# Identity products in TensorE's waits, fewer transposes on TensorE, and a planner with measured transfer figures

## The chip, the cores and the metric

The kernel runs on one core of a Trainium2 chip. The metric is the device time of one execution in microseconds (us). A profile's span is some 2 us shorter than the device time of the same execution, so spans are compared with spans and times with times. In the profile's lines PE is TensorE (matmuls), PEld its loading of weights, DVE is VectorE, ACT ScalarE, POOL GpSimd and SP the engine that issues most of the transfers; L295 is line 295 of that kernel. PSUM holds the tiles that this kernel's matmuls write; the program keeps eight of them and calls them banks.

## The reference

Four graph layers run one after the other on 32 graphs of 512 nodes and 128 features, all in FP32. Each layer normalises x, applies a ReLU, multiplies by the graph's 512 x 512 matrix or its transpose, and adds to x. Cut to what matters:

```python
h = maximum(layernorm(x), 0); x = x + L0(h, adj)   # one linear map, adj scaled by degrees
h = maximum(layernorm(x), 0); x = x + L1(h, adj)   # two aggregations (adj and adj.T), elu, tanh
h = maximum(layernorm(x), 0); x = x + L2(h, adj)   # four such layers; adj normalised by rows and by columns
h = maximum(layernorm(x), 0); x = x + L3(h, adj)   # a message step, then a GRU cell
return x
```

## The kernel before

The kernel is written as a list of operations for each graph ("batch"), and a planner in Python fixes one order for all engines before the program is built. The planner simulates the engines and the DMA queue with a duration for each operation, and starts on each engine the ready operation with the earliest due time.

The parts that the change touches are these. How a transfer is reckoned, and when a batch is due:

```python
PERIOD = 28.0                     # us from one batch's due time to the next one's
RATE, TRANSFER = 240.0, 1.3       # bytes per ns of the queue; us to landing
...
if kb:                            # op(): a transfer of kb thousand bytes
    o.us, o.land = max(us, kb / self.RATE), self.TRANSFER + land
...
due = o.batch * PERIOD if o.batch < B - 1 else (B - 2) * PERIOD + ENDING
o.key = (due - o.tail + o.later if o.rank is None else o.rank - 1e6, i)
```

The reserve of PSUM banks: an operation of a batch may take a new bank only if this many are left for each older unfinished batch:

```python
older = item[1].batch - min(unfinished)
if any(len(free[x.kind]) < ... + older * self.kept.get(x.kind, 0) for x in new):
    held.append(item); continue
...
plan = Plan(sb, psum, {"bank": 8, ...}, {"bank": 1, ...})
```

How h is turned (128 features on partitions in place of 128 nodes). In most batches VectorE transposes in blocks (0.71 us for a tile of 128 x 512 in the trace) and the tile goes out to memory and back in another order. In the first three and the last two batches TensorE does it, sixteen transposes of 128 x 128 a batch:

```python
at_ends = b < 3 or b >= B - 2

def transposed(h, name):
    if at_ends:
        for c in range(NC): ... nc.tensor.transpose(ps[:, c*P:(c+1)*P], h[:, c, :], ident)
        ... nc.scalar.copy(hT, ps)
        return hT
    t = turned(h, "turned")       # VectorE block transpose, four stores of 64 KB, a load of 256 KB
    ... nc.scalar.copy(hT, t in order)
```

And the spreading of the norms over all partitions:

```python
op("SP", 0.4, bounced, [inv], [bounce], kb=128)
op("SP", 0.4, spread, [bounce], [spaced], kb=512)       # DMA, 512 KB
op("ACT", t_act(2 * N), lambda: nc.scalar.copy(rows..., spaced...), [spaced], [rows])
```

At the end all operations are emitted in the planned order: `for o in plan.order(): o.emit()`.

## Time and profile before

| | before |
|---|---|
| device time, median of 3 (range) | 2331.95 us (2329.25 to 2332.02) |
| span of the profile, mean clock | 2328.9 us, 0.997 |
| TensorE busy | 2293.4 us |
| first real matmul | at 11.06 us |

The lines that matter are shown in the prediction below. They say that TensorE is the bound, that it is practically without a gap between 60 and 2180 us, and that what can be won lies in the first 60 us and around 2188 us. One line of TensorE's waits is added here: the group that waited, what released it, then us in total, times, and the longest. (Line numbers differ a little between kernels, since the edits add lines.)

```profile
PE ps_t L483 <- ACT h L447: 5.1, 3, 3.1
```

The three waits of the transposes for the normalised h (5.1 us, one of them 3.1) are the largest after the wait for the first weights. TensorE's clock in that trace: from the first matmul at 11.06 us to 16.46 us 25 records took 5.40 us, 0.216 each, where 12 later ones took 1.34 (21.72 to 23.06), 0.112 each; the granted clock was at half from 30.11 to 33.52 and from 54.00 to 60.83 us, then full to 2323.87 us.

To follow where time goes I cut each span into six pieces that add up to it, by my own count over TensorE's records in the traces. A record of 128, 256, 384 or 512 columns is typically followed by the next one 0.112, 0.216, 0.325 or 0.429 us later. The sum of these over all records that do real work is "real". Everything beyond is counted as lost where it occurs: in the start (before 60 us, after the first real matmul), the middle (60 to 2160 us) and the end. A product of the identity is counted wholly as lost. Before: 11.1 first matmul + 2279.9 real + 18.9 start + 4.3 middle + 7.2 end + 7.7 tail (last record to the end of the span), in sum 2329.1 (the last record's own spacing, 0.1 to 0.3, is in both real and tail).

### The profile page before, as it was taken

Reading aid. Unit: us, or ns where it says so; the run is one execution under the profiler, and the core shown is the slowest. Engines: PE = TensorE matmul, PEld = TensorE weight load, DVE = VectorE, ACT = ScalarE, POOL = GpSimd, SP = SyncE. Lnnn points to the kernel's source line nnn. Section 1 sums busy time; section 2 is a strip of 40 time slices with the busy share of each in tenths; the row PEclk is TensorE's granted clock in tenths of the full one; section 3 lists DMA queues with packets and bytes.
Section 4 is the critical chain, followed back from the end, with each engine's and each line's share of the span. In section 5 each row is a group of like instructions: output and inputs, shape, how many; then the busy total and the mean of one; then the engine's idle time right before and its main releaser. Section 6 shows DMA issues by size and latency. Waiting matters only on the chain.

```text
span 2328.9 us, 28035 instructions
## 1 busy us (share of the span) xinstructions
PE 2293.4 (98%) x9594; PEld 1438.1 (62%) x9594; DVE 1519.9 (65%) x4124; ACT 935.0 (40%) x2018; POOL 284.2 (12%) x218
## 2 busy tenths in 40 slices
PE   6999999999999999999999999999999999999998
PEld 4666666566665666666666666666656666666565
DVE  5556567666676776757766676666667667576754
ACT  7323434344343444434444333443434444344512
POOL 3001101111110111101111011111011111011101
PEclk9999999999999999999999999999999999999999
DMA  6202222323323133222233223232231332323100
GB/s 215 81 1 86 68 74 81 109 64 100 98 83 109 46 109 104 90 87 82 78 104 100 74 90 109 64 100 91 80 116 50 109 96 91 94 64 113 50 5 10
DMA packets 127295, 196.63 MB, mean 84 GB/s; under 512 B 18352, under 2 KB 75184, under 8 KB 127152
## 3 DMA queue, kind: packets, MB, share of 16 engines
q1 hardware_dynamic: 126864, 194.71, 27.2%
q8 instruction: 76, 1.25, 0.2%
q14 instruction: 67, 0.55, 0.1%
q10 hardware_dynamic: 288, 0.13, 0.0%
HBM read 157.95 MB, written 36.83 MB: 84 GB/s over the span
## 4 chain that ended last, share of the span: by engine, by line
PE 91%; DVE 3%; issue 2%; DMA 2%; ACT 1%; POOL 1%; SPq 0%; DVEq 0%; POOLq 0%; ACTq 0%
PE ps_agg L295 60%; PE ps_seven L566 12%; PE ps_sd L295 9%; PE ps_upd L295 3%; PE ps_gate L295 2%; PE ps_msg L295 1%; PE ps_lin L295 1%; PE ps_node L295 1%; DMA x<-in_x 0%; POOL inv L690 0%; ACT h L447 0%; DVE bn L419 0%; SPq L465 0%; DMA turned<-turn_turned 0%; DVE z L637 0%
## 5 line engine op out<-in xcount | busy, mean ns | idle before, releaser
L295 PE MATMUL ps_agg<-aT,sd 128*128 128x512 f32 x1024 | 509.6, 593 | 1.8 <-DVE sd L544 1.0
L295 PE MATMUL ps_agg<-a,sd 128*128 128x512 f32 x1024 | 489.4, 593 | 0.0
L435 POOL TENSOR_TENSOR sc<-v,neg_half 128x4 f32<-128x4 f32 (+1 forms) x128 | 170.0, 1328 | 1630.8 <-DVE v L422 1053.3
L295 PEld LDWEIGHTS ps_agg<-a,sd 128*128 128x128 f32 x1024 | 181.7, 190 | 158.3 <-issue 148.8
L447 ACT ACTIVATE h<-xr,nb,sc 128x128 f32<-128x128 f32 x384 | 158.2, 482 | 294.0 <-DVE nb L443 290.2
L295 PE MATMUL ps_agg<-f,w_sb 128*128 128x512 f32 x448 | 229.4, 594 | 0.0
L295 PEld LDWEIGHTS ps_agg<-aT,sd 128*128 128x128 f32 x1024 | 177.5, 191 | 75.1 <-issue 62.0
L295 PE MATMUL ps_sd<-w_sb,f 128*128 128x256 f32 x768 | 221.6, 381 | 1.8 <-ACT f L485 1.3
L566 PEld LDWEIGHTS ps_seven<-t_sb,s 128*128 128x128 f32 x1128 | 164.2, 191 | 67.9 <-issue 56.2
L295 PEld LDWEIGHTS ps_sd<-w_sb,f 128*128 128x128 f32 x768 | 137.5, 192 | 107.4 <-issue 85.0
L522 DVE TENSOR_TENSOR sd<-ps_sd,rf_sb 128x512 f32<-128x512 f32 x128 | 88.2, 689 | 145.2 <-PE ps_sd L295 144.5
L566 PE MATMUL ps_seven<-t_sb,s 128*128 128x128 f32 x1128 | 177.2, 275 | 0.0
L737 ACT ACTIVATE f<-ps_agg,cf_sb 128x512 f32<-128x512 f32 x128 | 87.4, 683 | 145.3 <-PE ps_agg L295 145.0
L295 PE MATMUL ps_agg<-aT,rep 128*128 128x512 f32 x256 | 130.9, 593 | 2.6 <-DVE rep L662 1.4
L295 PE MATMUL ps_agg<-a,rep 128*128 128x512 f32 x256 | 130.7, 592 | 0.0
L295 PE MATMUL ps_agg<-aT,msg 128*128 128x512 f32 x256 | 127.6, 593 | 0.0
L566 PEld LDWEIGHTS ps_seven<-w_sb,f 128*128 128x128 f32 x512 | 83.5, 191 | 55.7 <-issue 47.1
L690 POOL TENSOR_TENSOR inv<-stat,neg_half 128x8 f32<-128x8 f32 x32 | 64.7, 2022 | 370.5 <-DVE stat L689 370.5
L592 DVE TENSOR_TENSOR ev<-ps_seven,ev 128x512 f32<-128x512 f32 x94 | 64.6, 688 | 65.0 <-PE ps_seven L566 63.5
L607 ACT ACTIVATE sq<-a 128x512 f32<-128x512 f32 x128 | 79.9, 624 | 51.7 <-DMA a<-in_adj 50.3
L295 PE MATMUL ps_agg<-aT,h 128*128 128x256 f32 (+2 forms) x384 | 99.7, 380 | 0.0
L295 PEld LDWEIGHTS ps_agg<-f,w_sb 128*128 128x128 f32 x448 | 78.4, 191 | 27.8 <-issue 20.3
(142 smaller groups left out, 3781.9 us busy)
## 6 DMA issues: line engine op xcount, KB each, us to landing
aT<-in_adjt SPq DMA_DIRECT2D x124, 512.0 KB, 5.7
a<-in_adj SPq DMA_DIRECT2D x62, 512.0 KB, 5.5
turn_turned<-blk SPq DMA_DIRECT2D x324, 64.0 KB, 1.8
turned<-turn_turned SPq DMA_DIRECT2D x81, 256.0 KB, 2.7
spaced<-bounce SPq DMA_DIRECT2D x32, 512.0 KB, 4.8
x<-in_x SPq DMA_DIRECT2D x32, 256.0 KB, 2.8
out<-xo SPq DMA_DIRECT2D x30, 256.0 KB, 2.1
turn_f4r<-blk SPq DMA_DIRECT2D x108, 64.0 KB, 1.8
```

The costliest lines, as they stand in the source:

```text
L295: op("PE", t_mm(n), lambda: nc.tensor.matmul(out_of(ps.ap()), lhs(), rhs(), start=start, stop=stop), reads, [ps], later=later)
L435: op("POOL", t_pow(n), lambda: nc.gpsimd.tensor_tensor(inv.ap()[:, :n], v8.ap()[:, :n], neg_half[:, :n], op=ALU.pow), [v8, NH], [(inv, {0})])
L447: op("ACT", t_act(D, 2), lambda c=c: nc.scalar.activation(h.ap()[:, c, :], xin.ap()[:, c, :], AF.Relu, bias=nb.ap()[:, c:c + 1], scale=inv ...
L522: op("DVE", t_tt(N), lambda ps=ps, h=h: nc.vector.tensor_add(sd.ap()[:, 2 * h:2 * h + 2, :], ps.ap().rearrange("p (j v) -> p j v", j=2), s ...
L566: op("PE", t_mm(D), lambda j=j: nc.tensor.matmul(ps.ap()[:, k * H + j * D:k * H + (j + 1) * D], lhs()[:, j * P:(j + 1) * P], rhs(), start= ...
L592: op("DVE", t_tt(N), lambda: nc.vector.tensor_add(ev.ap(), bank_b.ap()[:, None, :H].to_broadcast([P, 2, H]), ev.ap()), [bank_b, ev], [ev])
L607: op("ACT", 0.73, lambda c=c: nc.scalar.activation(sq.ap(), a.ap()[:, c, :], AF.Copy, accum_out=stat.ap()[:, c:c + 1]), [(a, {c})], [sq, ( ...
L690: op("POOL", t_pow(2 * NC), lambda: nc.gpsimd.tensor_tensor(inv.ap(), stat.ap(), neg_half, op=ALU.pow), [stat, NH], [inv])
L737: op("ACT", t_act(N, 1), lambda ps=ps, i=i, f_new=f_new: nc.scalar.activation(f_new.ap(), ps.ap(), AF.Tanh, bias=cf_sb[:, i:i + 1]), [ps, ...
```

## The change

The intent: (1) where the planner foresees a wait of TensorE of over 0.7 us, products of the identity with itself are put into it, as many as it should hold, so that the clock stays up; (2) batches 2 and 30 are turned by way of VectorE and memory and no longer on TensorE; (3) the planner's figures for transfers are taken from the trace (it reckons 400 bytes per ns for the queue in place of 240, where the trace before has 404 to 411 GB/s between 10 and 20 us; and for a load 1.5 us plus its size at 175, which is 3.0 us for a turned tile of 256 KB, where that trace has a median of 2.7), batches are 30 us apart in place of 28, and two PSUM banks are reserved for each older batch in place of one.

```diff
-PERIOD = 28.0
+PERIOD = 30.0
...
-    RATE, TRANSFER = 240.0, 1.3
+    RATE, ALONE, TRANSFER, ISSUE = 400.0, 175.0, 1.5, 0.45
...
         if kb:
-            o.us, o.land = max(us, kb / self.RATE), self.TRANSFER + land
+            o.us = max(self.ISSUE, kb / self.RATE)
+            o.land = self.TRANSFER + kb / self.ALONE - o.us
...
+    WARM, COLD, RISE, SHORT = 0.2225, 0.428, 3.5, 0.7
+
+    def kept_warm(self, done, product, begin):
+        banks = {x for o in done for x in o.bufs if x.kind == "bank"}
+        out, at, cold = [], begin, self.RISE
+        for o in done:
+            if o.engine == "PE":
+                gap = o.ready - at
+                if gap > self.SHORT:
+                    n = int(min(gap, cold) / self.COLD + max(gap - cold - 0.1, 0.0) / self.WARM)
+                    cold = 0.0
+                    used = {x.slot for x in banks if x.since < o.ready and x.until > at - 0.1}
+                    slot = next((k for k in range(self.places["bank"]) if k not in used), None)
+                    if slot is not None:
+                        out.append((slot, n))
+                at = o.ready + o.us
+            out.append(o)
... (then emits them; a pair (slot, n) becomes n products)
-    plan = Plan(sb, psum, {"bank": 8, ...}, {"bank": 1, ...})
+    plan = Plan(sb, psum, {"bank": 8, ...}, {"bank": 2, ...})
...
-        at_ends = b < 3 or b >= B - 2
+        at_ends = b < 2 or b >= B - 1
...
+    def idle_products(slot, n):
+        ps = psum.tile([P, N], F32, name="ps_idle", tag=f"bank_{slot}", bufs=1)
+        for _ in range(n):
+            nc.tensor.matmul(ps[:, :P], ident, ident, start=True, stop=True)
...
-        for o in plan.order():
-            o.emit()
+        plan.kept_warm(plan.order(), idle_products, 1.3)
```

## The prediction

> **What bounds the kernel now.** I read the table of busy time first, then the slices, then the sums by stretch, and last TensorE's own list in order of time for the two stretches where it idles.
>
> ```profile
> PE 2293.4 (98%) x9594; PEld 1438.1 (62%) x9594; DVE 1519.9 (65%) x4124; ACT 935.0 (40%) x2018; POOL 284.2 (12%) x218
> ...
> PE   6999999999999999999999999999999999999998
> ...
> PE 91%; DVE 3%; issue 2%; DMA 2%; ACT 1%; POOL 1%; SPq 0%; DVEq 0%; POOLq 0%; ACTq 0%
> ```
>
> TensorE is busy for 2293.4 of 2328.9 us, only the first and last slices are not full, and 91% of the chain that ended last is matmuls. Nothing off TensorE can be worth much by itself. All that is left outside TensorE's busy time is 2328.9 - 2293.4 = 35.5 us, 1.5% of the span. The sums by stretch say where these lie (columns: stretch, its length, then busy time and instructions of PE, PEld, DVE, ACT, POOL, then granted clock, DMA share, GB/s):
>
> ```profile
> 0.00:60.00 60.00, 39.13 (x185) 29.45 (x186) 30.96 (x126) 43.08 (x112) 17.59 (x21) 0.92 0.62 214
> 60.00:2180.00 2120.00, 2117.03 (x8852) 1324.28 (x8850) 1407.62 (x3784) 851.82 (x1818) 250.23 (x175) 1.00 0.28 85
> 2180.00:2196.00 16.00, 13.43 (x50) 7.88 (x50) 10.39 (x37) 8.85 (x18) 5.45 (x4) 1.00 0.41 118
> 2196.00:2300.00 104.00, 102.67 (x402) 60.95 (x402) 53.38 (x127) 17.26 (x32) 2.01 (x2) 1.00 0.03 8
> 2300.00:2329.00 29.00, 21.14 (x107) 15.56 (x106) 17.58 (x53) 14.00 (x43) 8.88 (x17) 0.91 0.07 19
> ```
>
> The first 60 us hold 20.9 us of idle TensorE, the 2120 us after them only 3.0, the 16 us around 2188 hold 2.6, the next stretch 1.3, and the tail 7.9. The last is mostly the gate arithmetic and the store after the last matmul (ended at 2321.5 us). The clock is under full only at the two ends. In TensorE's list in order of time of the first 60 us (start, duration, what, idle before):
>
> ```profile
> 11.06 2.93 PE L295 MATMUL ps_fold<-raw 128*128 128x128 f32 x12 [11.06 <-DMA raw<-in_raw]
> ...
> 30.00 3.68 PE L295 MATMUL ps_sd<-w_sb,hT 128*128 128x256 f32 x8 [0.75 <-ACT hT L485]
> ...
> 55.43 1.63 PE L483 MATMUL ps_t<-ident,h 128*128 128x128 f32 x4 [3.07 <-ACT h L447]
> ```
>
> and of the stretch near the end:
>
> ```profile
> 2182.34 1.48 PE L483 MATMUL ps_t<-ident,h 128*128 128x128 f32 x4 [0.65 <-ACT h L447]
> ...
> 2191.39 1.89 PE L295 MATMUL ps_sd<-w_sb,hT 128*128 128x256 f32 x8
> ```
>
> The last line is the same eight records as those at 30.00: 1.89 us here, 3.68 us there. That is the clock: the early eight came after two waits and ran at half rate.
>
> [...] The cold stretch at 30 us does follow a stretch of transposes and waits, but this trace does not part the two. [...] a 128-column matmul here is two records, 24 of which take 2.68 us back to back (the chain has such a piece at 376.99), so 0.224 us for one. [...] the trace reaches 404 to 411 GB/s in the stretches 10 to 20 us. The planner's old 240 was too low, its new 400 fits.
>
> **The change, part by part.** (1) Transposes: the list of groups has 60 + 20 transposes, 16 for each of five batches; in the changed program's order there are 48, for three batches. 32 records of 0.11 us (0.112 us is the spacing in 2.68/24) leave TensorE: **3.6 us**. They go to VectorE (8 block transposes of 0.71 us, 5.7 us on an engine that is 65% busy) and to the DMA queue, where a turned tile lands about 1.8 + 2.7 us after it is issued. That is in two batches which have others beside them.
>
> (2) Products of the identity: the changed program's order has 60, in six places: 29 before the first real matmul, 14 before the first transposes, 6 before the first pair product, 3 somewhat later, 4 in the third batch or so, 4 near the end. None lies in the long middle. They take no time of their own where TensorE would wait anyway; they buy the clock. The cold excess now: the first 12 fold records took 2.72 us (11.06 to 13.78) where 12 later ones took 1.34 (21.72 to 23.06): 1.4. The bias folds after them took 2.4 us where half as many later took 0.6: 1.2. The eight at 30.00: 1.8. The four at 57.73 took 1.87 us to the next one, half of 1.73: 1.0, and what follows them until the clock rises at 60.8, 0.5. Sum **5.9 us**, all of it ahead of work that waits for TensorE. The 29 need no more time than there is: the identity is ready at 1.35 us and the first weights land at 11.06. With a rise after 5 us, that is some 12 products of 0.43 and 17 of 0.224, 9 us, ending before 11.06.
>
> (3) The new order: how many products the change puts into a wait is how long it expects the wait to be. Before 60 us these are 14 + 6 + 3 = 23, or 23 x 0.224 = 5.2 us; I add 1.5 us for waits too short to be filled. Now: 20.9 us less the 11.06 at the start, 9.8 us, and some 10 restarts at which a recorded matmul (593 ns for a 512-column record that follows the last by 429) is not overlapped, 0.16 us each: 11.4. Gain 11.4 - 6.7 = **4.7 us**. At the end: 2.6 + 1.3 us of idle time and some 7 restarts, 5.0 us, most of it around the transposes of the last batch but one, which go; the changed order expects one wait of 4 products, 0.9 us, and I add 0.6: gain **3.5 us**. The middle has 3.0 us idle; nothing to win, and it may gain or lose one.
>
> (4) Unchanged: 11.06 us before the first weights, because the first twelve transfers stand in the same order, and 7.4 us after the last matmul, because the last batch's gates are emitted in the same order.
>
> Sum: 3.6 + 5.9 + 4.7 + 3.5 = 17.7 us. Against it: products are fixed in number. Where the data come sooner than the planner expects, they hold TensorE up. I follow the first wait with durations of the trace: with warm folds and aggregation ahead of the bias folds, the aggregation ends near 16.8 us (now 20.0), the chain over the linear map, VectorE and the power on GpSimd to the transposes is some 8 us as now, so the transposes could start near 25; TensorE has work to 23.7 and then 3.1 us of products, to 26.8. That is 1.7 us too long, though still a microsecond before today's 27.77. I take off **2 us** for all such places, out of 6.9 us of products after the first 29. Left: 15.7, so 2332 - 16 = **2316 us**.
>
> **The rivals.** (a) The products are too many and become work: at worst 6.9 us, leaving a gain near 11, and 2321. For it speaks the first wait as just followed; against it, that some wait is there in each of these places today (1.4, 0.75 and 3.07 us in the list above and its neighbours). (b) The turned tiles of two more batches arrive late, because a tile's way over memory (VectorE, four stores, a load, ScalarE: some 6 us) is longer than over the array (some 1.5 us), and the start is when the queue is fullest (0.97 DMA share in 30 to 40 us). TensorE would then wait in the third batch and the last but one: perhaps 3 to 6 us, and 2320. Against it: the planner's figures for these transfers are at or above the trace's 1.8 and 2.7. (c) The reordering costs the middle something: the reserve of PSUM banks grows from one to two, and older batches get more preference; at 0.3 us a batch that is 9 us and would leave 2325. Against it: TensorE has 99.9% there and no wait above 0.8 us. (d) The order fits better than I allow and the waits vanish: at most 4 to 6 us more, 2310.
>
> **Range and chances.** From the sum with all rivals for it, 2308, to the sum with two against it, 2326. For a gain of over 2% it would have to come under 2286 us, 46 us less. All idle time (35.5), all cold excess (5.9) and all transposes taken out (3.6) are 45 us, and of that the 11.06 and the 7.4 can't go. So: faster 0.01, same 0.98, slower 0.01.
>
> **What would show it right or wrong.** Records of the idle product in the first 11 us and the clock up before the first fold; the eight records of the first pair product in some 1.9 us instead of 3.68; 48 transposes; TensorE's idle time in the first 60 us down from 20.9 to about 16 with the products counted as idle; the stretch before the last batch without its waits; the middle at 99.8% or more. It is wrong if the products before the first transposes end after the data are there by more than 2 us, if waits for turned tiles appear in the third batch or the last but one, or if the middle loses more than 3 us.

## The result, and the profile after

| | before | after |
|---|---|---|
| device time, median of 6 (range) | 2330.71 us (2329.25 to 2332.02) | 2319.77 us (2318.56 to 2322.74) |
| ratio of after to before, 95% interval | | 0.9955 (0.9942 to 0.9968) |
| span of the profile, mean clock | 2328.9 us, 0.997 | 2319.2 us, 0.998 |
| first real matmul | 11.1 | 11.1 |
| real | 2279.9 | 2276.3 |
| lost at the start (of it products) | 18.9 | 13.0 (5.5) |
| lost in the middle (products) | 4.3 | 9.1 (1.2) |
| lost at the end (products) | 7.2 | 2.0 (0.9) |
| tail | 7.7 | 7.7 |

A ratio is the mean time of one kernel's fast runs over that of the other's fast runs of the same rounds, so it is not quite the ratio of the medians. The outputs are correct. The time is 11 us shorter, 0.45%.

The table of busy time, TensorE's slices and the chain that ended last, of the changed kernel:

```profile
PE 2301.0 (99%) x9682; PEld 1446.3 (62%) x9682; DVE 1530.8 (66%) x4132; ACT 946.4 (41%) x2018; POOL 262.6 (11%) x218
...
PE   9999999999999999999999999999999999999998
...
PE 91%; DMA 3%; DVE 3%; ACT 2%; POOL 1%; SPq 0%; issue 0%; DVEq 0%; ACTq 0%; POOLq 0%
```

TensorE is busier (2301.0 against 2293.4 us) although it has less to do: the profile counts the products as busy. That is why the table above counts them as lost. The sums by stretch of the changed kernel, in the columns of the prediction's table:

```profile
0.00:60.00 60.00, 54.61 (x321) 44.10 (x322) 35.60 (x142) 46.15 (x122) 17.62 (x21) 0.97 0.73 261
60.00:2180.00 2120.00, 2115.10 (x8810) 1319.42 (x8809) 1417.11 (x3779) 859.94 (x1807) 230.43 (x175) 1.00 0.28 85
2180.00:2196.00 16.00, 16.00 (x73) 10.48 (x72) 9.59 (x38) 8.86 (x19) 3.67 (x3) 1.00 0.32 110
```

The start has filled up (39.13 to 54.61 us, much of it products), its granted clock went from 0.92 to 0.97, the stretch around 2188 us has no gap left. But the long middle went the other way: 2115.10 us busy where it had been 2117.03, although 1.2 us of products are in it. TensorE's list in order of time at the start (start, duration, what, count, idle before):

```profile
1.40 9.48 PE L864 MATMUL ps_idle<-ident 128*128 128x128 f32 x58 [1.40 <-POOL ident masks.py:199]
11.14 1.57 PE L326 MATMUL ps_fold<-raw 128*128 128x128 f32 x12 [0.27 <-DMA raw<-in_raw]
...
24.07 3.37 PE L864 MATMUL ps_idle<-ident 128*128 128x128 f32 x28
27.27 1.35 PE L514 MATMUL ps_t<-ident,h 128*128 128x128 f32 x4
28.46 1.50 PE L864 MATMUL ps_idle<-ident 128*128 128x128 f32 x12
29.80 1.89 PE L326 MATMUL ps_sd<-w_sb,hT 128*128 128x256 f32 x8
...
36.46 1.13 PE L326 MATMUL ps_agg<-aT,rep 128*128 128x512 f32 x2 [2.10 <-DVE rep L693]
...
38.67 1.91 PE L326 MATMUL ps_agg<-aT,rep 128*128 128x512 f32 x2
...
41.70 1.02 PE L326 MATMUL ps_agg<-aT,rep 128*128 128x512 f32 x2
```

58 records are 29 products. They end at 10.88 us, the first twelve folds take 1.57 us (2.93 before), and the eight records of the first pair product at 29.80 take 1.89 us (3.68 before). So far it is as intended. At 36.46 stands a wait of 2.10 us that the planner had not foreseen and into which it put no product; two aggregation records take 1.91 us at 38.67 and 1.02 at 41.70: the granted clock was 0.50 from 37.88 to 41.29 us.

What TensorE waited for at 36.46 can be read from the lists of ScalarE, GpSimd and VectorE:

```profile
31.14 2.06 ACT L735 COPY rows<-spaced 128x1024 f32<-128x1024 f32 x1 [0.89 <-DMA spaced<-bounce]
33.10 0.50 ACT L478 ACTIVATE h<-x,nb,sc 128x128 f32<-128x128 f32 x1
33.50 0.62 ACT L690 ACTIVATE rep<-sd 128x512 f32<-128x512 f32 x1
```

```profile
34.13 1.26 POOL L649 TENSOR_TENSOR diag<-aT,ident 128x512 f32<-128x512 f32 x1 [5.87 <-DMA aT<-in_adjt]
```

```profile
34.15 1.53 DVE L691 TENSOR_SCALAR rep<-rep 128x512 f32<-128x512 f32 x1 [1.73 <-ACT rep L690]
35.72 0.69 DVE L693 TENSOR_TENSOR rep<-rep,sd 128x512 f32<-128x512 f32 x1
36.33 0.42 DVE L691 TENSOR_SCALAR rep<-rep 128x512 f32<-128x512 f32 x1
```

ScalarE had to copy the spread norms first, and waited 0.89 us for them; `rep` stands behind that copy, which itself took 2.06 us. Then VectorE's step on `rep` took 1.53 us, where the same step takes 0.42 at 36.33: GpSimd's `diag` ran from 34.13 to 35.39, and VectorE's step ended 0.29 us after it. This was the slowest of the 64 such steps in the trace, whose median is 0.42. If the slow step came from its neighbour on GpSimd, 0.9 us of the 2.1 came from the transfer and some 1.1 (1.53 - 0.42) from the neighbour, by my estimate; no run parts the two.

In the middle TensorE's aggregation waited five times, 3.8 us in all, for `f` of ScalarE, which it had not done before:

```profile
PE ps_agg L326 <- ACT f L768: 3.8, 5, 1.1
```

One of these places, as VectorE, ScalarE and TensorE show it:

```profile
990.94 0.69 DVE L784 TENSOR_TENSOR xr<-xr,f4r 128x512 f32<-128x512 f32 x1 [1.63 <-DMA f4r<-turn_f4r]
```

```profile
995.18 1.65 ACT L478 ACTIVATE h<-xr,nb,sc 128x128 f32<-128x128 f32 x4 [1.46 <-DVE nb L474]
996.73 0.67 ACT L768 ACTIVATE f<-ps_agg,cf_sb 128x512 f32<-128x512 f32 x1
```

```profile
997.45 1.13 PE L326 MATMUL ps_agg<-f,w_sb 128*128 128x512 f32 x2 [1.06 <-ACT f L768]
```

A turned tile (`f4r`) came late, so the sum and its normalisation came late. ScalarE's four steps for `h` waited 1.46 us for that, and behind them stood `f`, whose aggregation had ended on TensorE at 994.16. TensorE needed `f` and stood for 1.06 us. ScalarE was idle for 1.46 us, the last 1.0 of them (994.16 to 995.18) with the input of `f` ready, and took the steps for `h` first. The late tile itself: in that stretch its load took 3.9 us beside the 512 KB spread. Times to landing of this tile over the whole run, before and after:

```profile
DMA to landing us min/median/max: 2.5/2.7/4.6
```

```profile
DMA to landing us min/median/max: 2.5/3.3/4.8
```

### The profile page after: what moved, and what is told of

It reads as the page before. It is cut to its first block, busy times and chain, and to the rows that moved or that the text cites.

```text
span 2319.2 us, 28279 instructions
## 1 busy us (share of the span) xinstructions
PE 2301.0 (99%) x9682; PEld 1446.3 (62%) x9682; DVE 1530.8 (66%) x4132; ACT 946.4 (41%) x2018; POOL 262.6 (11%) x218
## 3 DMA queue, kind: packets, MB, share of 16 engines
q8 instruction: 76, 1.25, 0.2%
## 4 chain that ended last, share of the span: by engine, by line
PE 91%; DMA 3%; DVE 3%; ACT 2%; POOL 1%; SPq 0%; issue 0%; DVEq 0%; ACTq 0%; POOLq 0%
PE ps_agg L326 61%; PE ps_seven L597 11%; PE ps_sd L326 9%; PE ps_upd L326 4%; PE ps_gate L326 2%; PE ps_msg L326 1%; DMA f4r<-turn_f4r 1%; PE ps_node L326 1%; PE ps_lin L326 1%; ACT h L478 1%; DMA turn_f4r<-blk 1%; POOL sc L466 1%; SPq L496 0%; ACT f L768 0%; DVE bn L450 0%
## 5 line engine op out<-in xcount | busy, mean ns | idle before, releaser
L326 PE MATMUL ps_agg<-a,sd 128*128 128x512 f32 x1024 | 482.4, 592 | 0.0
L466 POOL TENSOR_TENSOR sc<-v,neg_half 128x4 f32<-128x4 f32 (+1 forms) x128 | 157.8, 1233 | 1638.6 <-DVE v L453 1361.8
L597 PE MATMUL ps_seven<-t_sb,s 128*128 128x128 f32 x1128 | 168.1, 275 | 0.0
L735 ACT COPY rows<-spaced 128x1024 f32<-128x1024 f32 x32 | 66.1, 2064 | 164.9 <-DMA spaced<-bounce 164.9
L487 DVE STREAM_TRANSPOSE blk<-f 128x512 f32<-128x512 f32 x29 | 20.6, 711 | 144.2 <-ACT f L768 144.2
L597 PEld LDWEIGHTS ps_seven<-w_sb,f 128*128 128x128 f32 x512 | 75.9, 191 | 35.4 <-issue 27.7
L739 DVE TENSOR_TENSOR aT<-aT,rows 128x512 f32<-128x512 f32 x128 | 87.9, 687 | 14.7 <-PE ps_agg L326 14.6
L739 DVE TENSOR_TENSOR a<-a,rows 128x512 f32<-128x512 f32 x128 | 88.1, 689 | 13.6 <-PE ps_agg L326 13.5
```

Source lines behind the costliest of these rows:

```text
L326: op("PE", t_mm(n), lambda: nc.tensor.matmul(out_of(ps.ap()), lhs(), rhs(), start=start, stop=stop), reads, [ps], later=later)
L466: op("POOL", t_pow(n), lambda: nc.gpsimd.tensor_tensor(inv.ap()[:, :n], v8.ap()[:, :n], neg_half[:, :n], op=ALU.pow), [v8, NH], [(inv, {0})])
L487: op("DVE", t_tt(N), lambda: nc.vector.transpose(blk.ap().rearrange("p b (c r) -> p c b r", c=NC), m.ap().rearrange("p c (b s) -> p c b s" ...
L597: op("PE", t_mm(D), lambda j=j: nc.tensor.matmul(ps.ap()[:, k * H + j * D:k * H + (j + 1) * D], lhs()[:, j * P:(j + 1) * P], rhs(), start= ...
L735: op("ACT", t_act(2 * N), lambda: nc.scalar.copy(rows.ap().rearrange("p s (c n) -> p (s c) n", c=NC), spaced.ap().rearrange("p n k -> p k ...
L739: op("DVE", t_tt(N), lambda m=m, c=c, s=s: nc.vector.tensor_mul(m.ap()[:, c, :], m.ap()[:, c, :], rows.ap()[:, s, :]), [(m, {c}), rows], [ ...
```

## The experiments

Three parts of the change can be done alone: the **products** (P), the fewer transposes at the **ends** (E) and the planner's new figures (**rates**, spacing and reserve, together R). Theory one was that all of the gain is what I had reckoned: the ends 3.6 us and a little of their waits, the products the clock, and the new order the waits. Its rival was that the new order gains at the start and gives it back in the middle. All times are medians of five or six runs, unless said otherwise, and each ratio is to the kernel before on the same chip in the same rounds; one unit in the third decimal is 2.3 us, and an interval is some 3 us to each side.

### Each part alone, and without the products

**The changed kernel without products** (E and R): `plan.kept_warm(...)` back to `for o in plan.order(): o.emit()`.

> The changed kernel, its order kept, without the 60 products. If the products buy the clock: the fold and the first aggregation, and the eight records of the first pair product (1.89 us with products) run cold again (3.7 us), 3 to 5 us more than the changed kernel, so about 2323 to 2325. Rival, products overstay and cost what they buy: within 1 us of the changed kernel or faster, with the transposes at 27.27 us starting earlier.

Measured: 2324.3 us (2323.32 to 2326.27), ratio 0.9966 (0.9953 to 0.998). The products are worth some 2.6 us by the ratios and 4.5 by the medians in the changed order. In the trace the clock is low at the start up to 16.3 us and again from 29.9 to 33.4 (mean granted clock of the first 60 us 0.97). But the gain is not to be seen where it was meant: first matmul and start lose 23.8 us here and 24.1 with products. The changed kernel's lead (1.3 us at some 20 us) is gone at the end of the eight aggregations on `rep`, 44.79 us here and 45.13 there: the same wait for `rep`, 1.87 us before 37.85, brought no fall of the clock here. The two spans differ by 2.7 us, and the traces put that into the middle (12.4 against 9.1), where only four of the 60 products stand. What the products gain in this order is thus shown by the times alone.

**The kernel before with products** (P): only `kept_warm` and what it needs; 90 products, since the old planner foresees more waits.

> The kernel before with its own order and the products alone (90 of them, counted from its own planner). If cold clock cost 5.9 us as the prediction reckoned: 2325 to 2327, 4 to 6 us under the kernel before, with the pair product at 30 us in 1.9 instead of 3.7 us. Rival, the products hold up work that is ready: under 2 us gained.

Measured: 2326.27 us (2324.48 to 2327.76), ratio 0.9972 (0.996 to 0.9985), 6.5 us below before by the ratio. The mean granted clock of its first 60 us was 1.00, where the kernel before had 0.92.

**The kernel before with fewer transposes** (E):

```diff
-        at_ends = b < 3 or b >= B - 2
+        at_ends = b < 2 or b >= B - 1
```

> The kernel before with fewer transposes on TensorE alone (three batches at the ends in place of five). 32 records of 0.112 us are 3.6 us; with the waits around the transposes of the last batch but one (about 3 us) 5 to 7 us gained, 2324 to 2326. Rival, the turned tiles come late: waits for them in the third batch and the last but one, under 3 us gained.

Measured: 2323.05 us (2321.22 to 2323.93), ratio 0.9957 (0.9944 to 0.9969): as much as the whole change, from this one line. Of 7.7 us between the spans, 3.6 is real matmul time and 5.1 is lost less at the end (7.2 to 2.1); the start and the middle lost 0.1 and 1.0 more. The stretch around 2188 us in that kernel:

```profile
2180.00:2196.00 16.00, 15.67 (x62) 9.78 (x61) 9.44 (x27) 7.43 (x18) 1.65 (x1) 1.00 0.50 149
```

It had been 13.43 us busy. The waits went with the transposes. My reading is that near the end few batches are left to fill a wait for `h`, and that TensorE needs a tile that is turned elsewhere only later; no run tests this reading by itself.

### The planner's figures

**The transfer rates alone:** the lines with RATE, ALONE, TRANSFER and ISSUE, nothing else.

> The kernel before with the planner's new transfer rates and latencies alone. The middle is at 99.9% already, so 0 to 3 us either way: 2328 to 2333. Rival, the order is where the gain lies: 5 us or more gained.

Measured: 2344.9 us (2343.03 to 2345.78), ratio 1.0051 (1.0038 to 1.0064), slower by 12 us by the ratio. The start lost only 11.8 us in place of 18.9, but the middle lost 17.3 and the end 13.5. The top line of TensorE's waits, beside that for the first weights:

```profile
PE ps_t L484 <- ACT h L448: 8.9, 2, 6.3
```

**Spacing and reserve alone** (three rounds): PERIOD 30 and two banks, with the old rates.

> The kernel before with the planner's new spacing of batches (30 for 28) and two reserved PSUM banks per older batch alone, its old transfer rates kept. If the spacing and the reserve are what repairs the 13 us that the new rates cost alone, they should cost by themselves, because the same planner with the new ends and products puts 36 products (8 us) into every third batch: 2350 to 2420. Rival, they do nothing by themselves: within 4 us of the kernel before.

Measured: 2445.51 us (2444.48 to 2447.54), ratio 1.0486 (1.0471 to 1.05), slower by 113 us. In every third batch TensorE waited long, twice:

```profile
PE ps_sd L295 <- ACT f L488: 43.2, 8, 6.5
PE ps_agg L295 <- POOL diag L618: 22.7, 8, 2.8
```

The two are 66 us in 16 waits, and the mean granted clock of the span was 0.983 (before 0.997). Why just every third batch is not shown; that the two changes are only good with the new rates is.

**All of the planner's figures** (R), without products and with the old ends:

> The kernel before with all three of the planner's changes (rates, spacing, reserve), without products and with the transposes of before. If the parts add up: the changed kernel without products (2324.3) with the 8.5 us of the transposes back, 2331 to 2334, so the new order gains nothing. Rival, the new order is worth some us by itself: under 2329.

Measured: 2334.04 us (2332.67 to 2334.37), ratio 1.0005 (0.9992 to 1.0017). So the two halves, each bad alone, together gain nothing: 6.5 us less is lost at the start (12.4), 8.3 more in the middle (12.6). This is the rival's picture. The waits in the middle are those of the changed kernel, for the same `f`:

```profile
PE ps_agg L296 <- ACT f L738: 6.8, 9, 1.3
```

**Products and ends on the old planner** (P and E), with 79 products:

> The kernel before with products and fewer transposes and its old planner figures. If the parts add up: 2331.5 - 5.2 - 8.5 = 2318, so as fast as the changed kernel or 1 to 3 us faster. Rival, the changed kernel needs the new figures for the others to pay: over 2322.

Measured: 2319.65 us (2315.9 to 2320.58), ratio 0.9943 (0.9928 to 0.9957). That is the changed kernel's time, without any of the new figures. (The profiled execution was a fast one of it, 2316.96 us.) In its sums by stretch the middle is as it was before:

```profile
60.00:2180.00 2120.00, 2116.33 (x8825) 1322.42 (x8826) 1412.57 (x3796) 849.13 (x1809) 256.41 (x175) 1.00 0.28 86
```

**The changed kernel with one bank reserved:** `{"bank": 2, ...}` back to `{"bank": 1, ...}`.

> The changed kernel with one reserved PSUM bank instead of two. Its planner puts 3 products into a wait of every one of 27 middle batches (81 x 0.224 = 18 us). If the second reserved bank is what the new figures need: 2330 to 2340. Rival, the reserve makes no difference on the chip, and only the products are added: up to 2338 too but with the products the only added time; or none: 2318 to 2322.

Measured: 2343.94 us (2342.57 to 2344.67), ratio 1.0055 (1.0043 to 1.0068), 24 us above the changed kernel. With the new rates the reserve is needed: without it the planner itself foresees more waits, puts 138 products in (60 in the changed kernel), 82 of them in the middle, and the middle loses 34.9 us, 18.9 of them in products.

The seven combinations of P, E and R that were run (the eighth, P and R without E, was not), with what each trace lost:

| kernel | ratio to before | median us | first matmul + start | middle | end |
|---|---|---|---|---|---|
| before | 1 | 2330.7 to 2332.0 | 30.0 | 4.3 | 7.2 |
| P | 0.9972 | 2326.27 | 24.6 | 6.6 | 6.8 |
| E | 0.9957 | 2323.05 | 29.8 | 5.3 | 2.1 |
| R | 1.0005 | 2334.04 | 23.5 | 12.6 | 7.5 |
| P, E | 0.9943 | 2319.65 | 22.9 | 5.4 | 3.0 |
| E, R | 0.9966 | 2324.3 | 23.8 | 12.4 | 1.8 |
| P, E, R (the change) | 0.9955 | 2319.77 | 24.1 | 9.1 | 2.0 |

By the ratios the ends gain 7 to 10 us in each pair that differs only in them, the products 3 to 7, and the new figures cost 1 to 3, which is no more than an interval's half-width and so not shown to differ from nothing. The middle of every order by the old planner lost 4.3 to 6.6 us, that of every order by the new one 9.1 to 12.6; kernels with the same order differ by 2 or 3 us in this column, so the difference between the two groups is more than the scatter.

### Is it the unforeseen waits?

My account of the changed kernel's start was that the planner thinks the spread of the norms lands too early. If that is the cause, telling it so should move the ScalarE copy behind `rep` and take the 2.1 us wait and the cold stretch away.

**The spread reckoned 2 us later, in all batches:**

```diff
-        op("SP", 0.4, spread, [bounce], [spaced], kb=512)
+        op("SP", 0.4, spread, [bounce], [spaced], kb=512).land += 2.0
```

> The changed kernel with one figure of the planner changed: the spread of the column scales is said to land 2 us later, so ScalarE's copy of it is queued behind other work. If that copy standing ahead of the first features in ScalarE's queue costs the 2.3 us wait at 34 us and the cold clock after it (1.7 us), and similar waits in the middle: 2314 to 2317. Rival, what is lost is due to products: within 2 us of the changed kernel.

Measured: 2333.7 us (2333.24 to 2334.41), ratio 1.0006 (0.9993 to 1.0018). The start did what it should. In TensorE's list the aggregation that had started at 36.46 us starts at 34.30 without a wait:

```profile
34.30 1.02 PE L326 MATMUL ps_agg<-aT,rep 128*128 128x512 f32 x2
```

No cold stretch follows (mean granted clock of the first 60 us 1.00), and the eight aggregations are done at 41.17 us in place of 45.13. The start lost 10.9 us in place of 13.0. But the middle lost 23.3, with this on top of TensorE's waits:

```profile
PE ps_agg L326 <- ACT f L768: 12.5, 14, 1.6
```

The figure holds for 32 batches, and in those in the middle it made a worse order. It was also a wrong figure: the planner had 4.4 us (1.5 + 512/175), and in the changed kernel's trace the spread took 5.3 us in the first batch but 4.0 in the median of all (3.3 to 5.3). So 2 us more is too much even for the first batch; 0.9 more there, as measured, was not tried.

**The same for the first batch alone** (`+= 2.0 if b == 0 else 0.0`):

> The changed kernel with the spread of the column scales said to land 2 us later for the first batch alone. If the copy of it ahead of the first features in ScalarE's queue is what costs the 2.3 us wait at 34 us and 1.7 us of cold clock after it, and the loss of the previous experiment lay in the middle only: 2314 to 2317, 3 to 5 us under the changed kernel, with the start as in the previous experiment. Rival, another wait takes its place: within 1.5 us of the changed kernel.

Measured: 2326.94 us (2324.96 to 2327.41), ratio 0.998 (0.9968 to 0.9993). I had hoped to get the start for nothing; the run missed that. The start lost 11.7 us, but the middle 15.6, with nine waits for the same `f` (7.5 us), although no figure of a batch in the middle was touched. A list order is a chain: another start makes another order in all that follows.

**That, and the load of `f4r` reckoned 1.5 us later**, to take away the wait shown at 990.94 us:

```diff
-            op("SP", 0.4, lambda: nc.sync.dma_start(mT.ap(), bounce.tile), [bounce], [mT], kb=256)
+            op("SP", 0.4, lambda: nc.sync.dma_start(mT.ap(), bounce.tile), [bounce], [mT], kb=256).land += 1.5 if name == "f4r" else 0.0
```

> The same, and the planner is told that the turned fourth features land 1.5 us later, about what they take while the spread is in flight (3.9 against 2.6 us). If the repeated 1 us waits in the middle (ScalarE's tanh queued behind a normalisation that waits for that transfer) come from this figure: the middle loses 2 us or less instead of 4.9, so 2310 to 2314. Rival, the order moves the wait to another place each batch: 2316 or more.

Measured: 2326.13 us (2325.36 to 2326.9), ratio 0.9979 (0.9966 to 0.9993). The waits for `f` behind the normalisation went, as foreseen, but the middle still lost 15.7 us. The waits are now these:

```profile
PE ps_agg L326 <- DVE sd L553: 5.5, 15, 0.9
PE ps_sd L326 <- ACT hT L519: 3.2, 4, 1.8
```

The rival held: the wait moves elsewhere. That `f4r`'s late landing makes the waits for `f` in the changed order fits the trace and this run; that mending it gains time is refuted.

### Which of the products count?

**P and E on the old planner with the first 33 products alone**, the 46 in later waits left out. This was the last run.

> Before's planner with the fewer transposes and only the first 33 products of the identity, those ahead of the first real matmul; the 46 in later waits are left out. Without products this kernel's order took 2323.05 us (0.9957 of before), with all 79 it took 2319.65 (0.9943). Theory A, that the warm clock at the first fold is all that the products buy: 2319 to 2320.5 us, ratio 0.994 to 0.995, and the first pair products and what follows the first waits are at full rate or lose no more than they did with all products. Rival B, that the products in the later waits carry the clock over the waits before 40 us: 2321 to 2323, and the eight records of the first pair product at some 30 us are again near 3.7 us instead of 1.9.

Measured: 2318.03 us (2317.27 to 2321.92), ratio 0.9949 (0.9935 to 0.9962). The time is theory A's: no difference from all 79 can be shown (2319.65, ratio 0.9943). But the mark that I had given for rival B is there too. The eight records of the first pair product, here and with all 79 products:

```profile
28.11 3.78 PE L323 MATMUL ps_sd<-w_sb,hT 128*128 128x256 f32 x8 [0.75 <-ACT hT L513]
```

```profile
27.97 1.99 PE L323 MATMUL ps_sd<-w_sb,hT 128*128 128x256 f32 x8
```

So the later products do hold the clock: with them no record before 2310 us ran at half rate after the warm-up, without them the clock was low from 27.4 to 34.3 and from 54.7 to 58.2 us (mean granted clock of the first 60 us 1.00 against 0.91). In the traces that makes 3.9 us at the start (first matmul + start 26.8 against 22.9). The kernel with all products lost as much elsewhere: 3.0 us more in the middle and at the end, of it 2.1 in products near the end. Whether that is chance of these two profiles or a price of the products stays open; the times do not part the two kernels. The first products here also show that they can stay too long: the clock rose only at 7.0 us (5.4 with all 79), 33 products then took 10.27 us, and the first fold started at 11.73 us in place of 10.98, without a wait for its data.

## Why the prediction was right

The time, 2319.77 us, lies in the range, 3.8 us above the number. That is in part luck. Of the terms, the start came out 4.7 us short and the middle 4.8 us worse; against these 9.5 us stand 1.7 more at the end and the 2 us taken off for products that stay too long, which did not come. The rest, some 6 us, was within a range of 18 us. Between the two spans, 9.7 us are 3.6 + 5.9 - 4.8 + 5.2, less 0.1 for the first matmul and roundings.

- **What bounds the kernel:** right. TensorE is at 99%, and what could be won was at the two ends.
- **Transposes, 3.6 us:** right, 2279.9 to 2276.3. That VectorE and the queue would hide the turned tiles was right at the ends, where no wait for them showed.
- **Warm clock at the start, and fewer waits there, 5.9 + 4.7 us:** mis-sized. Measured 5.9 for both; split by the granted clock of each record, by my count, 4.0 for the clock (5.7 to 1.7) and 1.9 for waits with the products in them (13.2 to 11.3). My mark for the waits failed: TensorE's idle time in the first 60 us with the products counted as idle was to be about 16, and is 20.6 (60 - 54.61 + 15.2 of products). The new order alone shortens the waits by 4.2 (13.2 to 9.0); with products in them, 1.9 of that is left. The records that I had named are warm (1.57 and 1.89 us), but I took the planner's foreseen waits for the whole of the waits. The 2.10 us wait at 36.46 was not among them, and after it the clock fell for 3.4 us, which cost 1.7.
- **Transposes and the clock:** the prediction noted that the slow stretch at 30 us followed transposes and waits, and that its trace does not part the two. No run parts them either. With the ends alone the clock fell at 27.8 us, after 3.4 us with 1.87 us busy, in part with transposes, but in the changed kernel it fell after 1.44 us of ordinary matmuls as well (last section). In the kernel before it fell at 30.11, after 3.41 us with 1.48 us busy, the records of four transposes making up 1.31 of it; another 3.41 us with 1.31 us of four transposes, 2.47 us busy in all (2180.51 to 2183.92), were not followed by a fall. Whether a transpose counts for the clock as other matmuls do is not shown.
- **The end, 3.5 us:** mis-sized the other way, 5.2; with the ends alone 5.1.
- **The middle, "nothing to win, and it may gain or lose one":** this is the step that failed. It lost 4.8 us in the changed kernel (1.2 in four products at 266 us, where I had said that none lies), 8.3 with the figures alone. By my own mark, "the middle loses more than 3 us", the account was wrong here. My rival (c), that the reordering costs the middle, held in part, at half of its 9 us. My argument against it, that TensorE has 99.9% there, was no argument: an order that is good to 99.9% has only room to get worse.
- **Products that stay too long, 2 us off:** not seen in the changed kernel. The first wait held 3.2 us of products and the data came 0.1 to 0.2 us before their end, because the step before the normalisation took 1.23 us (at 25.33) in place of the 0.16 it takes at 994.98. That step too ran beside GpSimd's `diag` (25.27 to 26.54). The danger was real, as the last run shows with 0.7 us.
- **Rival (b), turned tiles late:** not at the ends, where I had looked for it, but in the middle, as part of (c).
- **The new order as a gain:** not one, within intervals of some 3 us. On the old planner, products and ends give the same time.

No version tried is faster than the changed kernel beyond the intervals. The kernel with products and ends on the old planner and the one with the first products alone are equal to the changed kernel, with less changed.

## What to carry to other kernels

When every engine follows one fixed order, better figures in the planner are not a safe gain: they make another order, and one place mended in one batch may be paid for in thirty. Try each part of such a change alone before shipping the sum; here one line (where to transpose) brought 7 to 10 of the 11 us and three new figures brought nothing. Products of the identity before the first real matmul are cheap, but count them so that they end before the data land, since with products from 1.4 us on the clock rose at 5.4 us (products and ends), 7.0 (the first products alone) and 7.15 (the changed kernel).

## What the traces show of the clock, and of slow steps on VectorE

- Waits of 2.10 us (changed kernel, 34.4 to 36.5) and 2.26 us (ends alone, 42.6 to 44.9) were each followed by a stretch at half clock that lasted 3.4 us; one of 1.25 us (products and ends, 40.0 to 41.25) was not. The 3.4 us before the fall and the 3.4 at half clock, in the changed kernel (sums by stretch: stretch, length, busy time and instructions of TensorE first, the clock third from the end):

```profile
34.50:37.90 3.40, 1.44 (x4) 0.72 (x5) 3.37 (x6) 3.40 (x10) 0.90 (x1) 1.00 1.03 401
37.90:41.30 3.40, 3.40 (x6) 1.31 (x5) 2.36 (x5) 3.40 (x12) 0.00 (x0) 0.50 1.05 394
```

  and the stretch with the shorter wait, in the kernel with products and ends, after which the clock stayed up:

```profile
37.90:41.30 3.40, 2.15 (x8) 0.85 (x6) 0.55 (x1) 3.40 (x7) 0.00 (x0) 1.00 0.76 296
41.30:44.70 3.40, 3.40 (x30) 3.37 (x31) 3.40 (x10) 3.40 (x11) 0.00 (x0) 1.00 0.02 8
```

  So the 3.4 us before the fall were not idle throughout: they were 42% busy (1.44 of 3.40). In the other kernel 3.4 us that were 63% busy (2.15 of 3.40) had no fall after them. In the traces of the kernel before and of the changed kernel all changes of the granted clock lie a whole number of 3.41 us apart: half clock from 30.11 to 33.52, from 54.00 to 60.83 and from 2323.87 us in the one, from 37.88 to 41.29 and from 2314.56 us in the other. Cut at these places, by my count, the stretches of 3.41 us at full clock with a fall after them were 17 to 43% busy (41% in the changed kernel at 34.46 us; 34 and 43% before, at 50.59 and 26.70 us), and the least busy one without a fall after it 58% (before, 1.97 of 3.41 us at 2194.16). With the ends alone 3.4 us that were 55% busy (1.87 us, from 24.4 us) had a fall after them, so the two traces set no limit for other kernels; a record's length is also in part modelled.
- Beside a GpSimd step of 1.26 us a VectorE step on one input of 512 columns took 1.53 us in place of 0.42, and beside one of 1.27 us one with two inputs of four columns 1.23 in place of 0.16. Both GpSimd steps were `diag`; that they are the cause no run shows by itself.
